# A convolution and two state space layers: half of delta·u·B moved to ScalarE and TensorE, one ring of PSUM work banks, the layer's begin in pieces

## The chip, the cores and the metric

The kernel runs on one NeuronCore of a Trainium2 chip. TensorE (PE) multiplies matrices and transposes 128x128 blocks into PSUM; VectorE (DVE), ScalarE (ACT) and GpSimd (POOL) work on 128 partitions; SyncE (SP) starts DMAs. The metric is the device time of one execution in microseconds (us). All arithmetic is in float32.

## The reference

The input `x` has 4 images of 128 rows, 128 columns and 128 channels. Two residual layers follow one another, each behind a group norm over 32 groups:

```
x = x + L0(gn(x))      # deformable 3x3 sampling, depthwise 3x3, pointwise, 2 channel groups
x = x + L1(gn(x))      # two Mamba blocks over sequences: one image row, 128 positions, 128 channels
```

L0 predicts 18 offsets a position, samples the normed image bilinearly at 9 shifted points, and convolves. A Mamba block with 256 inner channels d and 16 states n computes

```
u, res  = split(h @ in_w);  u = silu(causal_conv4(u) + cb)
dt, B, C = split(u @ xw);   delta = softplus(dt @ dtw + dtb)
s[t,d,n] = exp(delta[t,d] * A[d,n]) * s[t-1,d,n] + delta[t,d]*u[t,d] * B[t,n]
y[t,d]   = sum_n s[t,d,n] * C[t,n] + u[t,d] * D[d]
h        = (y * silu(res)) @ ow
```

The products delta·u·B and the recurrence over t, for 4 x 128 rows, 2 blocks, 256 channels and 16 states, are what the change is about.

## The kernel before

**Layer 0.** `stats_part` reads four rows of x, transposes them and takes their statistics; `norm_part` makes scale and bias; `table_part` writes the normed image to DRAM as a table in which one entry holds the 2x2 neighbourhood of a position (8 writes of 128 KB a part). `prep` computes offsets, weights and indices for 8 rows. Then for each block of 4 rows (32 an image) and each of 9 units, `gather` issues 8 indirect DMAs from GpSimd into two `gt` tiles (`NGT` = 4 buffers), `sample` weights them on DVE (`gw`, line 382), transposes and sums them on PE (`p`) and copies them with ACT (`s`, line 396); for 5 of the 9 units `add_up` (line 415) issues the fused depthwise and pointwise matmuls into `acc`. A float32 matmul appears in the trace as two records, a transpose as one.

**Layer 1.** A job is one block of four image rows (512 positions, `TB`) and one Mamba block: 64 jobs an image, 256 in all. Channels lie on partitions, in two halves c. `pre` computes u, silu(res) (`g`), B and C (stored to DRAM as `bcd`), delta (`de`) and delta·u (`du`); softplus alternates between ACT and DVE (lines 538 to 550). `main` goes through eight steps q of two states n. In a step SP loads B and C of the two states, broadcast to all partitions (`bc`, two times 512 KB); ACT writes exp(delta·A) into one of three `da` tiles (line 580), whose first column of every row is zero so that the recurrence starts anew; DVE multiplies du by B into `hs` (line 586, once a state), runs the recurrence as one scan over 2048 elements (line 592) and multiplies by C (line 596); PE transposes the result into `y` (two PSUM banks), adding all states up (16 transposes a step, helper line 128). After eight steps DVE multiplies by `g` (line 607), PE transposes back and multiplies by `ow`. `pre` of the next job stands ahead of `main` of the present one in the text.

**Order of the work.** Image 0's layer 0 runs alone. After it, layer 0 of image b+1 and layer 1 of image b advance by turns, 288 units against 512 steps, layer 0 a little ahead; layer 1 of image 3 runs alone at the end. Statistics, norm and tables of image b+1 are spread over the units of layer 0 of image b (`todo`). The text of the program gives a priority only: the framework's planner models the engines and issues, on each engine, the earliest instruction in the text among those whose inputs and buffers it takes to be ready. The engines then run their queues in that fixed order. PSUM has eight banks: two for layer 0's work (`ps`), two for `acc` (`psa`), two for layer 1's work (`ps1`), two for `y`.

Of the kernel before, what the change touches and what calls it, by code (L numbers as in the profile page):

```python
# [24 lines left out]
NGT = 4  # L25
# [38 lines left out]
def block_kernel(ctx: ExitStack, tc: tile.TileContext, a: dict, out: bass.AP):  # L64
# [27 lines left out]
    ps = ctx.enter_context(tc.tile_pool(name="l0ps", bufs=2, space=PSUM))  # L92
# [3 lines left out]
    ps1 = ctx.enter_context(tc.tile_pool(name="l1ps", bufs=2, space=PSUM))  # L96
# [39 lines left out]
    dwb = loadw("dwb", [P, NT], pool=p2, tag="ot")  # L136
# [21 lines left out]
    dpar = loadw("dpar", [P, NL, NC], pool=p2, tag="ot")  # L158
# [4 lines left out]
    cvw = loadw("cvw", [P, NL, DCONV, NC * P], pool=p2, tag="hs")  # L163
    for l in range(NL):
        nc.vector.tensor_tensor(
            inc[:, l], cvw[:, l], inw[:, l].unsqueeze(1).to_broadcast([P, DCONV, NC * P]), ALU.mult
        )
# [23 lines left out]
    def norm_part(b):  # L191
# [3 lines left out]
        for nm, v in (("s", scale), ("b", bias)):  # L195
            dg = small.tile([P, P], F32, tag="dg", name=f"dg_{nm}_{b}")
            nc.vector.tensor_scalar(dg, ident, v, None, ALU.mult)
            pr = ps.tile([P, 512], F32, tag="t", name=f"prow_{nm}_{b}")
            nc.tensor.matmul(pr[:, 0:P], ones, dg, start=True, stop=True)
            row = small.tile([P, P], F32, tag=f"row_{nm}", name=f"row_{nm}_{b}")  # L200
            nc.scalar.copy(row, pr[:, 0:P])
            rows.append(row)
# [223 lines left out]
    def layer0(b):  # L426

        todo = []
        if b + 1 < B:
            todo += [lambda j=j: stats_part(b + 1, j) for j in range(NJ)]  # L430
            todo += [lambda: norm_part(b + 1)]
            todo += [lambda j=j: table_part(b + 1, j) for j in range(NJ)]
# [30 lines left out]
    das = [cw.tile([P, NC, NQ, SR, P], F32, name=f"da{i}") for i in range(NDA)]  # L463
# [14 lines left out]
    def load_x1(blk, nm):  # L478
# [3 lines left out]
        return t  # L482

    def pre(st, l):
# [25 lines left out]
        for i in range(SR // 2):  # L510
# [7 lines left out]
            tc.keep_in_program_order(nc.scalar.activation(g[:, 2 * i : 2 * i + 2], px, AF.Silu))  # L518
        pdb = ps1.tile([P, TB], F32, tag="t", name=f"pdb_{nm}")
# [7 lines left out]


        de = p2.tile([P, NC, TB], F32, tag="de", name=f"de_{nm}", bufs=2)
        du = p2.tile([P, NC, TB], F32, tag="du", name=f"du_{nm}", bufs=2)  # L530
        es, pdts = [], []
        for c in range(NC):
# [4 lines left out]
            e = p2.tile([P, TB], F32, tag="e", name=f"e_{nm}_{c}", bufs=2)  # L537
            nc.scalar.activation(e, pdt, AF.Abs)
            nc.scalar.activation(e, e, AF.Exp, scale=-1.0)
            es.append(e)  # L540
            pdts.append(pdt)
        for c in range(NC):
            e = es[c]
            w1 = p2.tile([P, TB], F32, tag="w1", name=f"w1_{nm}_{c}")
            nc.scalar.activation(w1, e, AF.Identity, bias=1.0)
            nc.scalar.activation(du[:, c], w1, AF.Ln)  # L546
            nc.vector.scalar_tensor_tensor(e, w1, 1.0, e, op0=ALU.subtract, op1=ALU.subtract)  # L547
            nc.vector.scalar_tensor_tensor(de[:, c], pdts[c], 0.0, e, op0=ALU.max, op1=ALU.subtract)  # L548
        nc.vector.tensor_tensor(de, de, du, ALU.add)  # L549
        nc.vector.tensor_tensor(du, de, u, ALU.mult)  # L550
        st.update(u=u, g=g, delta=de, du=du, bcd=bcd)

    def main(st, l):
# [5 lines left out]
        for i in range(SR):  # L559
            for c in range(NC):  # L560
# [3 lines left out]
                )  # L564
        for q in range(NS // NQ):
            bc = []
            for w in range(2):
                t = p2.tile([P, NQ, TB], F32, tag=f"bc{w}", name=f"bc{w}_{nm}_{q}", bufs=2)
                n0 = w * NS + q * NQ
                nc.sync.dma_start(t, st["bcd"][n0 : n0 + NQ, :].partition_broadcast(P))  # L570
                bc.append(t)
# [3 lines left out]
            nc.scalar.copy(da.rearrange("p c n s t -> p (c n s) t")[:, :, 0], zero)  # L575
            for c in range(NC):
                dv = st["delta"][:, c].rearrange("p (s t) -> p s t", s=SR)
                for n in range(NQ):
                    s = q * NQ + n
                    nc.scalar.activation(  # L580
                        da[:, c, n, :, 1:], dv[:, :, 1:], AF.Exp, scale=aneg[:, l, c, s : s + 1]
                    )
            hs = p2.tile([P, NC, NQ, TB], F32, tag="hs", name=f"hs_{nm}_{q}")

            for n in range(NQ):
                nc.vector.scalar_tensor_tensor(  # L586
                    hs[:, :, n, :], st["du"], ones[:, 0:1],
                    bc[0][:, n].unsqueeze(1).to_broadcast([P, NC, TB]),
                    op0=ALU.mult, op1=ALU.mult,
                )  # L590
            df = da.rearrange("p c n s t -> p (c n s t)")
            nc.vector.tensor_tensor_scan(  # L592
                df, df, hs.rearrange("p c n t -> p (c n t)"), zero[:, 0:1], ALU.mult, ALU.add
            )
            dc = da.rearrange("p c n s t -> p c (n s t)")
            nc.vector.scalar_tensor_tensor(  # L596
                dc, dc, ones[:, 0:1],
                bc[1].rearrange("p n t -> p (n t)").unsqueeze(1).to_broadcast([P, NC, NQ * TB]),
                op0=ALU.mult, op1=ALU.mult,
            )  # L600
            for c in range(NC):
                for n in range(NQ):
                    for i in range(SR):
                        add_transposed(y[:, i, c], da[:, c, n, i, :], False, q == NS // NQ - 1 and n == NQ - 1)
# [15 lines left out]
        else:  # L620
# [8 lines left out]
            ot = p2.tile([P, SR, P], F32, tag="ot", name=f"ot_{nm}")  # L629
# [11 lines left out]
    def layer1():  # L641
        pre(*jobs[0])
        for i, job in enumerate(jobs):
            if i + 1 < len(jobs):
                pre(*jobs[i + 1])
            yield from main(*job)
# [101 lines left out]
```

## Time and profile before

| | us |
|---|---|
| median of 3 runs | 26,681.26 (26,681.15 to 26,698.94) |
| the profiled execution's own time | 26,698.06 |
| its span | 26,696.0 |
| DVE busy | 23,505.8 (88%) |
| PE busy | 19,620.5 (73%) |
| POOL busy | 16,017.0 (60%) |
| ACT busy | 11,605.1 (43%) |

The first gather starts at 319.7 us, the first scan of layer 1 at 3471.2 us, and the last gather at 21,045.0 us. A group's row gives line, engine, operation, output and inputs with their shapes, the count, then busy us and the mean duration in ns of one, then the idle time of the engine just ahead of such instructions and who ended most of it. A row of a stretch gives, for each engine, its busy us and its number of instructions, then TensorE's granted clock as a share of full speed, the share of time the DMA engines were busy, and GB/s. Time in which an engine waits is not busy, but a GpSimd gather held up while it runs is. Ends of matmuls are modelled, so PE's busy time is somewhat above what its array needs.

### The profile page before, as it was taken

The numbers are of one execution on the slowest core, as the hardware profiler recorded it, in microseconds if no ns is written. First come the engines' busy times: TensorE is split into PE (matmuls) and PEld (weight loads), VectorE is DVE, ScalarE is ACT, GpSimd is POOL, SyncE is SP. The second block draws the span as 40 slices with busy tenths as digits, with TensorE's granted clock in tenths as the row PEclk, the third lists the DMA queues.
The fourth block names the chain that finished last, engine by engine and source line by source line (L and its number), as shares of the span: only waits on it lengthen the run. The fifth ranks groups of instructions, "written<-read, shape, count | busy, mean of one in ns | idle before, by whom it ended". The sixth has DMA issues, their size and how long they took to land. (4 is left out here: it accounts for less than half of the span.)

```text
span 26696.0 us, 294801 instructions
## 1 busy us (share of the span) xinstructions
PE 19620.5 (73%) x112196; PEld 13523.4 (51%) x112196; DVE 23505.8 (88%) x14042; ACT 11605.1 (43%) x18181; POOL 16017.0 (60%) x9222
## 2 busy tenths in 40 slices
PE   4777788878888778887888778888888655555555
PEld 3444455555555555555555555555555443434344
DVE  2232289999999999999999999999999999999999
ACT  0000044444444544444444454444445455555554
POOL 4777777878877767888878667877878400000000
PEclk7888888888999888888998888899998866666666
DMA  5363344456544444455544444444444333333332
GB/s 146 114 172 107 106 147 155 157 170 183 165 153 154 149 144 155 158 173 181 164 154 153 148 143 151 156 150 152 154 154 156 130 107 106 107 106 107 107 106 102
DMA packets 1994602, 3804.53 MB, mean 143 GB/s; under 512 B 771796, under 2 KB 1116116, under 8 KB 1993053
## 3 DMA queue, kind: packets, MB, share of 16 engines
q1 hardware_dynamic: 1550812, 2577.13, 29.9%
q0 software_dynamic: 442368, 1208.55, 14.4%
q8 instruction: 880, 14.42, 0.2%
q14 instruction: 542, 4.43, 0.0%
HBM read 3567.63 MB, written 217.05 MB: 142 GB/s over the span
## 5 line engine op out<-in xcount | busy, mean ns | idle before, releaser
L364 POOL DMA_INDIRECT gt<-table,idx x9216 | 16016.3, 1738 | 5031.5 <-issue 2999.5
L592 DVE TENSOR_TENSOR_SCAN da<-da,zero,hs 128x2048 f32<-128x2048 f32 x2048 | 9176.1, 4481 | 351.7 <-ACT da L580 247.1
L128 PE MATMUL y<-ident,da 128*128 128x128 f32 x32768 | 5252.0, 326 | 3956.1 <-DVE da L596 3955.4
L580 ACT ACTIVATE da<-de,aneg 128x508 f32<-128x508 f32 x8192 | 5550.5, 712 | 5605.2 <-PE y L128 5351.0
L128 PEld LDWEIGHTS y<-ident,da 128*128 128x128 f32 x32768 | 4682.4, 171 | 4953.3 <-DVE da L596 2520.6
L415 PE MATMUL acc<-s,wc 128*64 128x256 f32 (+3 forms) x38400 | 6403.2, 453 | 761.4 <-ACT s L396 760.9
L586 DVE SCALAR_TENSOR_TENSOR hs<-du,ones,bc 128x1024 f32<-128x1024 f32 x4096 | 5093.2, 1277 | 0.0
L415 PEld LDWEIGHTS acc<-s,wc 128*64 128x64 f32 x38400 | 3352.0, 145 | 3083.2 <-issue 1446.2
L596 DVE SCALAR_TENSOR_TENSOR da<-da,ones,bc 128x2048 f32<-128x2048 f32 x2048 | 4807.9, 2348 | 25.9
L382 DVE TENSOR_TENSOR gw<-gt,wt 128x1024 f32<-128x1024 f32 x2304 | 2786.4, 1213 | 2133.3 <-DMA gt<-table,idx 1500.9
L128 PE MATMUL p<-ident,gw 128*128 128x128 f32 x18432 | 2724.3, 299 | 1714.1 <-DVE gw L382 1706.7
L128 PEld LDWEIGHTS p<-ident,gw 128*128 128x128 f32 x18432 | 2292.8, 154 | 2329.3 <-DVE gw L382 1752.7
L396 ACT COPY s<-p 128x512 f32<-128x512 f32 x1152 | 668.6, 581 | 3989.8 <-PE p L128 3982.0
L501 PE MATMUL pu<-hp,inc 128*128 128x512 f32 x4096 | 1808.3, 593 | 0.0
L580 ACT ACT_TABLE_LOAD x1016 | 1303.5, 1283 | 16.8 <-PE y L128 5.7
L501 PEld LDWEIGHTS pu<-hp,inc 128*128 128x128 f32 x4096 | 751.2, 188 | 865.9 <-issue 865.2
L508 ACT ACTIVATE u<-pu,w_cvb 128x512 f32<-128x512 f32 x512 | 324.6, 684 | 1468.9 <-PE y L561 1461.4
L561 PEld LDWEIGHTS y<-ddiag,u 128*128 128x128 f32 x4096 | 579.5, 200 | 192.0 <-issue 192.0
L612 PE MATMUL pyg<-ident,g 128*128 128x128 f32 x2048 | 353.9, 328 | 425.7 <-DVE g L607 424.8
L546 ACT ACT_TABLE_LOAD x500 | 641.5, 1283 | 8.9
L561 PE MATMUL y<-ddiag,u 128*128 128x128 f32 x4096 | 612.1, 284 | 0.0
L263 PE MATMUL pof<-xn,w_offw 128*64 128x512 f32 x2304 | 585.0, 613 | 20.0 <-ACT xn L257 12.0
(118 smaller groups left out, 11036.3 us busy)
## 6 DMA issues: line engine op xcount, KB each, us to landing
bc<-bcd SPq DMA_DIRECT2D x4096, 512.0 KB
gt<-table,idx POOLq DMA_INDIRECT x9216
table<-xt SPq DMA_DIRECT2D x984, 128.0 KB
xt<-in_x SPq DMA_DIRECT2D x124, 320.0 KB
xr<-in_x SPq DMA_DIRECT2D x128, 256.0 KB
x<-xo SPq DMA_DIRECT2D x128, 256.0 KB
x1t<-x SPq DMA_DIRECT2D x128, 256.0 KB
x1t_o<-x SPq DMA_DIRECT2D x128, 256.0 KB
```

The lines of the kernel that those rows point to most:

```text
L128: nc.tensor.matmul(o, v, ident, is_transpose=True, start=start, stop=stop, skip_group_check=True)
L364: nc.gpsimd.indirect_dma_start(out=gt[:, v, r], out_offset=None, in_=flat, in_offset=bass.IndirectOffsetOnAxis(ap=idx[:, ri, o : o + 1], a ...
L382: nc.vector.tensor_tensor(gw.rearrange("p r s v c -> p (r s) v c"), gts[h].rearrange("p v r (s c) -> p (r s) v c", c=CG), wv.unsqueeze(3). ...
L396: nc.scalar.copy(st[:, :, 1 : W + 1], p4)
L415: nc.tensor.matmul(accs[b, j + i0][CG * g : CG * g + CG, q : q + rb - ra, :], wc[sl, v, e, :], st[p + 4 * g if p < 4 else 8][sl, ra:rb, kx ...
L501: nc.tensor.matmul(px.rearrange("p (s t) -> p s t", s=SR), inc[:, l, j, c * P : (c + 1) * P], h[:, :, j : j + P], start=(j == 0), stop=(j ...
L546: nc.scalar.activation(du[:, c], w1, AF.Ln)
L561: nc.tensor.matmul(y[:, i, c], st["u"][:, c, i * P : (i + 1) * P], ddiag[:, l, c, :], start=(i % 2 == 0 and c == 0), stop=False, skip_grou ...
L580: nc.scalar.activation(da[:, c, n, :, 1:], dv[:, :, 1:], AF.Exp, scale=aneg[:, l, c, s : s + 1])
L586: nc.vector.scalar_tensor_tensor(hs[:, :, n, :], st["du"], ones[:, 0:1], bc[0][:, n].unsqueeze(1).to_broadcast([P, NC, TB]), op0=ALU.mult, ...
L592: nc.vector.tensor_tensor_scan(df, df, hs.rearrange("p c n t -> p (c n t)"), zero[:, 0:1], ALU.mult, ALU.add)
L596: nc.vector.scalar_tensor_tensor(dc, dc, ones[:, 0:1], bc[1].rearrange("p n t -> p (n t)").unsqueeze(1).to_broadcast([P, NC, NQ * TB]), op ...
```

## The change

- In every step the product delta·u·B of the second state is no longer made by DVE. `pre` transposes `du` once a job (`dut`: positions on partitions) and B likewise (`bt`); in the transposed form B is one number a partition, so ACT multiplies 128x256 pieces by it (`xs`, four a state), and PE transposes them back into one PSUM bank (`psx`), from where the scan reads them, once for each half c.
- The scan of a step is split: the first state from `hs` as before (1024 elements), the second in two scans of 512 from PSUM. B is loaded for the first state only (`bs`), C for both (`cs`).
- For image 3 (`in_last`), whose layer 1 runs alone, GpSimd makes `xs` of the first state as well, `hs` and `bs` are gone, all four scans read PSUM, and two of them use the two `acc` banks, which are free then.
- The multiply by C is a `tensor_tensor` in place of a `scalar_tensor_tensor` with a factor of one.
- `pre` becomes a generator of pieces, run after the steps of the previous job. Softplus is done by ACT on both halves together, max(x,0) by a Relu; DVE's part (four instructions on 1024 elements) comes two steps later.
- One ring of three PSUM banks serves both layers' work in place of two and two; `NGT` is 3 in place of 4.
- Statistics, norms and tables of images 1, 2 and 3 are all spread over layer 0 of image 0.
- Some tiles change the tag under which they share memory; one weight load (`cvw`) comes in two halves.

```diff
-NGT = 4
+NGT = 3
...
-    ps = ctx.enter_context(tc.tile_pool(name="l0ps", bufs=2, space=PSUM))
+    ps = ctx.enter_context(tc.tile_pool(name="ps", bufs=3, space=PSUM))
...
-    ps1 = ctx.enter_context(tc.tile_pool(name="l1ps", bufs=2, space=PSUM))
+    ps1 = ps
+    psx = ctx.enter_context(tc.tile_pool(name="l1psx", bufs=1, space=PSUM))
...
     for l in range(NL):
+        cvw = p2.tile([P, DCONV, NC * P], F32, tag="hs", name=f"w_cvw_{l}")
+        nc.sync.dma_start(cvw, a["cvw"][:, l])
...
-        if b + 1 < B:
-            todo += [lambda j=j: stats_part(b + 1, j) for j in range(NJ)]
-            todo += [lambda: norm_part(b + 1)]
-            todo += [lambda j=j: table_part(b + 1, j) for j in range(NJ)]
+        for i in range(1, B) if b == 0 else ():
+            todo += [lambda i=i, j=j: stats_part(i, j) for j in range(NJ)]
+            todo += [lambda i=i: norm_part(i)]
+            todo += [lambda i=i, j=j: table_part(i, j) for j in range(NJ)]
...
+    def in_last(blk):
+
+        return blk * SR // H == B - 1
...
             tc.keep_in_program_order(nc.scalar.activation(g[:, 2 * i : 2 * i + 2], px, AF.Silu))
+        yield
...
+        pbt = ps1.tile([P, SR, XP], F32, tag="t", name=f"pbt_{nm}")
+        for i in range(SR):
+            nc.tensor.transpose(pbt[:, i, :], dbl[:, i * P : (i + 1) * P], ident[0:XP, 0:XP])
+        st["bt"] = p2.tile([P, SR, NS], F32, tag="bt", name=f"bt_{nm}", bufs=2)
+        nc.scalar.copy(st["bt"], pbt[:, :, DTR + 1 : DTR + 1 + NS])
+        yield
...
-            e = p2.tile([P, TB], F32, tag="e", name=f"e_{nm}_{c}", bufs=2)
-            nc.scalar.activation(e, pdt, AF.Abs)
-            nc.scalar.activation(e, e, AF.Exp, scale=-1.0)
-            es.append(e)
-            pdts.append(pdt)
-        for c in range(NC):
-            e = es[c]
-            w1 = p2.tile([P, TB], F32, tag="w1", name=f"w1_{nm}_{c}")
-            nc.scalar.activation(w1, e, AF.Identity, bias=1.0)
-            nc.scalar.activation(du[:, c], w1, AF.Ln)
-            nc.vector.scalar_tensor_tensor(e, w1, 1.0, e, op0=ALU.subtract, op1=ALU.subtract)
-            nc.vector.scalar_tensor_tensor(de[:, c], pdts[c], 0.0, e, op0=ALU.max, op1=ALU.subtract)
+            nc.scalar.activation(e[:, c], pdt, AF.Abs)
+            nc.scalar.activation(de[:, c], pdt, AF.Relu)
+        nc.scalar.activation(e, e, AF.Exp, scale=-1.0)
+        nc.scalar.activation(w1, e, AF.Identity, bias=1.0)
+        nc.scalar.activation(du, w1, AF.Ln)
+        nc.scalar.activation(w1, w1, AF.Identity, bias=-1.0)
+        yield
+        yield
+        nc.vector.tensor_tensor(e, w1, e, ALU.subtract)
+        nc.vector.tensor_tensor(de, de, e, ALU.subtract)
         nc.vector.tensor_tensor(de, de, du, ALU.add)
         nc.vector.tensor_tensor(du, de, u, ALU.mult)
+        dut = p2.tile([P, SR, NC * P], F32, tag="dut", name=f"dut_{nm}", bufs=2)
+        for k in range(SR // 2):
+            pt = ps1.tile([P, 2, NC, P], F32, tag="t", name=f"pdu_{nm}_{k}")
+            for i in range(2):
+                for c in range(NC):
+                    o = (2 * k + i) * P
+                    nc.tensor.transpose(pt[:, i, c, :], du[:, c, o : o + P], ident)
+            nc.scalar.copy(dut[:, 2 * k : 2 * k + 2], pt.rearrange("p s c d -> p s (c d)"))
...
+            turned = {}
+            for n in range(0 if last else 1, NQ):
+                s = q * NQ + n
+                for i in range(SR):
+                    if i % 2 == 0:
+                        xs = p2.tile([P, 2, NC * P], F32, tag="xs", name=f"xs_{nm}_{s}_{i}", bufs=3)
+                        turned[n, i] = xs
+                    bv = st["bt"][:, i, s : s + 1]
+                    if n:
+                        nc.scalar.activation(xs[:, i % 2], st["dut"][:, i], AF.Copy, scale=bv)
+                    else:
+                        nc.gpsimd.tensor_scalar(xs[:, i % 2], st["dut"][:, i], bv, None, ALU.mult)
+
+            def scan_turned(n, c):
+                pool, tag = (psa, "acc") if last and (n + c) % 2 else (psx, "x")
+                px = pool.tile([P, SR, P], F32, tag=tag, name=f"px_{nm}_{q}_{n}_{c}")
+                for i in range(SR):
+                    nc.tensor.transpose(px[:, i, :], turned[n, i - i % 2][:, i % 2, c * P : (c + 1) * P], ident)
+                dn = da[:, n, c].rearrange("p s t -> p (s t)")
+                nc.vector.tensor_tensor_scan(dn, dn, px.rearrange("p s t -> p (s t)"), 0.0, ALU.mult, ALU.add)
+
+            if last:
+                for n in range(NQ):
+                    for c in range(NC):
+                        scan_turned(n, c)
+            else:
+
+                hs = p2.tile([P, NC, TB], F32, tag="hs", name=f"hs_{nm}_{q}")
                 nc.vector.scalar_tensor_tensor(
-                    hs[:, :, n, :], st["du"], ones[:, 0:1],
-                    bc[0][:, n].unsqueeze(1).to_broadcast([P, NC, TB]),
+                    hs, st["du"], ones[:, 0:1], bs.unsqueeze(1).to_broadcast([P, NC, TB]),
                     op0=ALU.mult, op1=ALU.mult,
                 )
...
+                scan_turned(1, 0)
+                d0 = da[:, 0].rearrange("p c s t -> p (c s t)")
+                nc.vector.tensor_tensor_scan(
+                    d0, d0, hs.rearrange("p c t -> p (c t)"), 0.0, ALU.mult, ALU.add
+                )
+                scan_turned(1, 1)
+            dc = da.rearrange("p n c s t -> p n c (s t)")
+            nc.vector.tensor_tensor(dc, dc, cs.unsqueeze(2).to_broadcast([P, NQ, NC, TB]), ALU.mult)
...
     def layer1():
-        pre(*jobs[0])
+        for _ in pre(*jobs[0]):
+            pass
         for i, job in enumerate(jobs):
-            if i + 1 < len(jobs):
-                pre(*jobs[i + 1])
-            yield from main(*job)
+
+            nxt = pre(*jobs[i + 1]) if i + 1 < len(jobs) else iter(())
+            for _ in main(*job):
+                next(nxt, None)
+                yield
+            for _ in nxt:
+                pass
```

## The prediction

> **What bounds the kernel now.** I read the 40 slices first, for stages, then one table of busy times by stage, then the costliest groups, the waits, and the order of time where a wait needed its cause.
>
> ```profile
> DVE  2232289999999999999999999999999999999999
> POOL 4777777878877767888878667877878400000000
> PEclk7888888888999888888998888899998866666666
> ```
>
> Three stages show. In A (0 to 3430 us) image 0's layer 0 runs alone, with GpSimd (POOL) the busiest of the vector engines and VectorE (DVE) at 2 tenths. In B (to 21,050 us, the last gather) layer 1 of images 0 to 2 runs beside layer 0 of images 1 to 3. In C layer 1 of image 3 runs alone, and TensorE's granted clock drops.
>
> ```profile
> core 0: us, PE busy (x) PEld busy (x) DVE busy (x) ACT busy (x) POOL busy (x), PEclk, DMA share, GB/s
> 400.00:2400.00 2000.00, 1590.65 (x9911) 970.70 (x9912) 582.10 (x674) 151.50 (x268) 1548.25 (x1484) 0.88 0.47 132
> 5400.00:21000.00 15600.00, 12500.77 (x73564) 8599.82 (x73563) 15247.58 (x9079) 7541.39 (x11893) 12047.88 (x6101) 0.89 0.49 157
> 22000.00:26000.00 4000.00, 2097.48 (x9502) 1603.67 (x9500) 3798.31 (x1871) 2038.60 (x3096) 0.00 (x0) 0.70 0.31 107
> ```
>
> DVE is busy 97.7% of B and 95% of C: it is the bound of both. TensorE (PE) is at 80% in B, ScalarE (ACT) at 48% in B and 51% in C. Stage A is paced by POOL: 1484 gathers in 2000 us, 1.35 us each. The scan counts by stage give the number of state steps (two of the 16 states each):
>
> ```profile
> 3430.00:21050.00 17620.00, 6755.10 (x1508) 0.89 0.49 157
> 21050.00:26696.00 5646.00, 2421.01 (x540) 0.70 0.31 106
> ```
>
> So a step costs 17,620 / 1508 = 11.68 us in B and 10.46 in C. What DVE spends it on:
>
> ```profile
> L592 DVE TENSOR_TENSOR_SCAN da<-da,zero,hs 128x2048 f32<-128x2048 f32 x2048 | 9176.1, 4481 | 351.7 <-ACT da L580 247.1
> L586 DVE SCALAR_TENSOR_TENSOR hs<-du,ones,bc 128x1024 f32<-128x1024 f32 x4096 | 5093.2, 1277 | 0.0
> L596 DVE SCALAR_TENSOR_TENSOR da<-da,ones,bc 128x2048 f32<-128x2048 f32 x2048 | 4807.9, 2348 | 25.9
> L382 DVE TENSOR_TENSOR gw<-gt,wt 128x1024 f32<-128x1024 f32 x2304 | 2786.4, 1213 | 2133.3 <-DMA gt<-table,idx 1500.9
> ```
>
> The idle columns say that DVE hardly waits for anyone once layer 1 runs; the longest wait of C is for ScalarE's exponentials where layers meet (table of waits of C):
>
> ```profile
> DVE da L592 <- ACT da L580: 151.3, 48, 5.6
> ```
>
> That cover is what the change spends: PE and ACT now enter DVE's own chain, so their queues matter. The order of time shows PE's queue in B:
>
> ```profile
> 8061.95 4.48 DVE L592 TENSOR_TENSOR_SCAN da<-da,zero,hs 128x2048 f32<-128x2048 f32 x1
> 8062.57 7.97 PE L415 MATMUL acc<-s,wc 128*64 128x256 f32 x56
> 8063.16 4.03 POOL L364 DMA_INDIRECT gt<-table,idx  x1 [0.30 <-issue]
> 8070.47 1.96 PE L128 MATMUL y<-ident,da 128*128 128x128 f32 x16
> 8071.21 1.94 ACT L580 ACTIVATE da<-de,aneg 128x508 f32<-128x508 f32 x3 [8.97 <-PE y L128]
> ```
>
> Layer 0's add_up goes through PE in one piece of 8 us; the transposes of y stand behind it, and ACT waits 9 us for them. DVE does not feel it, as three da buffers lie between.
>
> **The change, part by part.**
>
> *DVE work of a step in B.* One of two hs multiplies goes: two in a row take 2.47 us, one 1.28, so -1.19. The multiply by C becomes a plain tensor_tensor; at 1024 elements that form has 1.214 us against 1.277, so -0.07. One scan of 2048 (4.48) becomes one of 1024 and two of 512 that read PSUM, which the trace lacks. L586 and L596 give a DVE instruction a fixed part of about 0.21 us; with that the scan costs 2.09 ns per element, so 2.34 + 2 x 1.27 = 4.89; neighbours overlap by 0.08 us (2 x 1.277 against 2.47). I take +0.25, between +0.2 and +0.45 (no overlap where the scan waits for PE). Reading PSUM is nearly free by a row: 682 ns at L548 (input in PSUM) against 678 at L547. Softplus: four instructions of 0.68 become two of about 1.21, -0.3 a layer, -0.04 a step. Statistics and tables of images 2 and 3 leave B: 64 x (0.69 + 0.82 + 0.81) = 148 us, -0.10 a step. Sum -1.15; times 1508, **-1,735 us**.
>
> *Waits it adds in B.* The scans of the second state use one PSUM bank: four transposes, scan, four transposes, scan. Ahead of the first lie the C multiply and hs (3.5 us) as cover, ahead of the second only the scan of 1024 (2.3 us). Four transposes need about 0.7 us, so PE is in time unless it is inside an add_up. Each add_up has 30 matmuls (60 records); there are 5 a row block, 160 an image, 480 in B. If an 8 us piece starts just before the second four, DVE waits 8 + 0.7 - 2.3 = 6.4 us; if it starts just after them, the scan of 1024, scan, multiply and next hs (7 us) hide all but 1.7. DVE can also fill in gw (2.4 us a unit). I take 2 us each, bounds 0 and 6.4: **+960** (0 to 3,070). PE itself has room: y's 16 transposes take 1.96 us, so 8 more are 1 us a step, and the turned du and B add 0.15; busy 9.4 of 11.7 becomes 10.5 of about 11.2, so little slack remains. ACT gains four multiplies of 256 elements a step; nearest row is the 128x260 copy, 0.405 us, so 0.4 to 0.5 each, plus some 3 us a layer (two Relus, two copies of the turned du, less work on joined tiles) and minus two table loads of 1.283: 5.6 us a step becomes about 7.3, hidden.
>
> *GpSimd and DMA in B.* A gather beside a scan waits for its end, above; beside DVE work that reads PSUM it does not:
>
> ```profile
> 4221.39 1.21 DVE L607 TENSOR_TENSOR g<-y,g 128x1024 f32<-128x1024 f32 x1
> 4221.45 0.95 POOL L364 DMA_INDIRECT gt<-table,idx  x1 [0.30 <-issue]
> ```
>
> So the short scans should free POOL, which now needs 1.97 + 0.3 us a gather, 15,700 of 17,620. With three gather buffers in place of four this hides at nothing; if POOL is not freed, it fills 93% of the shorter stage and gw comes late, up to +300. B is broadcast for one state, not two: 256 of 1024 KB a step go, from a queue that was not awaited. Three work banks for both layers instead of two and two: some 2.3 tiles a step with 3 to 4 us each are one bank in use on average; hidden, up to +200 if not.
>
> *Stage C.* Both hs go (-2.47), four scans of 512 in place of 4.48 (+0.45), the multiply -0.07: -2.09 a step, -16.7 a layer, with softplus -17. A layer of C takes 4000 / 48 = 83.3 us, 79.1 of it DVE; DVE falls to 62. ACT, 42.5 a layer, gains 32 x 0.4 to 0.5 and the 3 us, less 2.6: 55.5 to 58, over 90% of that. The other half is turned by GpSimd: four multiplies of 256 elements a step; the nearest POOL row is a select of 128 elements, 0.29 us, so 0.4 to 0.6 each, far under a step. DVE's idle time of 4.2 us a layer I raise to 7, because ACT works in blocks and xs has three buffers: 69 us, -14.3; times 64, **-915**, and -30 for the 28 steps that still have image 2's form.
>
> [...] The rows: 16 transposes take 1.96 us in B, but in C
>
> ```profile
> 24000.36 3.37 PE L128 MATMUL y<-ident,da 128*128 128x128 f32 x16 [5.75 <-DVE da L596]
> ```
>
> behind 5.75 us of idleness. They do run at full rate in B; whether a stage that is mostly transposes raises its own clock is not shown. [...]
>
> *Stage A* takes the 64 parts of images 2 and 3. With table traffic (1400 to 1800 us) 291 gathers started in 400 us, otherwise 300: 3% over some 450 us an image, +28. DMA share was 0.77 there, so packing three images' tables in stays under one. With three buffers a gather waits for the gw two tiles (10 us) back, which is done. The split weight load adds some 10. **+40**, up to +300.
>
> Sum: -1,735 + 960 - 945 + 40 = -1,680, from the profiled 26,698 to 25,018; the median run is 17 below it: **25,000 us**, own range 24,400 to 25,700.
>
> **Rivals.**
> 1. *No new waits*: the scheduler places transposes well. B -1,735, C -17 x 64 = -1,090: 23,860. For it: PE has 20% free. Against: the 8 us piece ahead of y.
> 2. *PE eats stage B's gain*, waits of 3.6 us an add_up, or C runs at the cold clock: 25,700 to 26,500, centre 26,000.
> 3. *Slower*: DVE waits at the single bank. Place: second four transposes behind add_up; price 6.4 us x 480 = 3,070, and C gains 600 only as ACT or PE binds: 26,681 + 1,335 - 600 + 40 = 27,450. It decides from (1,735 + 945 - 40) / 480 = 5.5 us an add_up. For it: ACT's 9 us above. Against: gw work fills, and nearly every piece must fall badly.
> 4. *It does not do what it says* for time: gains and waits cancel within 0.2% (53 us, about what a measurement can tell), 26,680.
>
> **How the numbers follow.** Chances: forecast 0.48, no waits 0.12, B eaten 0.20, slower 0.17, cancel 0.03. So faster 0.80, same 0.03, slower 0.17. The range 23,900 to 26,900 leaves out half of rival 1 and most of rival 3.
>
> **What would show it.** Right: scans of 512 at 1.2 to 1.35 us; DVE waiting for transposes some 1,000 us in B, mostly behind L415's successor; ACT above 85% busy in C; gathers' mean below 1.7 us; stage A ending near 3,470; granted clock of C near 0.8. Wrong: DVE's wait for transposes above 2,600 us, gw waiting for gathers by hundreds, C's clock at 0.7 with PE the last to end, or a scan from PSUM well above 1.4 us.

## The result, and the profile after

The changed kernel takes **28,220.88 us** (median of 4 runs, 28,203.61 to 28,242.33) where the kernel before takes 26,685.15 (4 runs beside them): a ratio of **1.0575, 95% interval 1.0557 to 1.0593**. It is slower by 5.8%. The forecast was 25,000, its range ended at 26,900; both missed, and in sign.

The profiled execution took 28,215.46 us, its span is 28,213.7. First the slices of the page of the changed kernel, each about 705 us long:

```profile
PE   5778788888888788888888788888888777777777
DVE  2333388888888888888888888888888866666666
POOL 4777765655555365655555365655555344444444
PEclk7889899999999899999999899999999888888888
```

The row of DVE had nines from slice 7 to the end, and now has eights in B (layer 1 beside layer 0) and sixes in C (layer 1 of image 3 alone). DVE has less to do and the kernel takes longer, so DVE stands idle more than before. The same three stretches as before the change (the third lies later because stage C begins later):

```profile
core 0: us, PE busy (x) PEld busy (x) DVE busy (x) ACT busy (x) POOL busy (x), PEclk, DMA share, GB/s
400.00:2400.00 2000.00, 1601.97 (x10153) 983.31 (x10149) 665.63 (x796) 152.61 (x273) 1546.73 (x1484) 0.89 0.59 160
5400.00:21000.00 15600.00, 13018.78 (x80708) 9278.54 (x80707) 12804.31 (x9304) 8874.47 (x16101) 8856.96 (x5704) 0.92 0.39 121
24000.00:28000.00 4000.00, 2951.97 (x15210) 2275.76 (x15210) 2747.16 (x2029) 2429.17 (x4302) 1822.10 (x1444) 0.82 0.16 53
```

In B DVE went from 15,248 to 12,804 us busy in 15,600, and no other engine is full: PE has 83%. In C nobody is above 74%. Where no engine is busy all the time, what sets the pace must be looked for in the waits between engines.

Cut at the first scan and the last gather, the spans are these (a step is two states of one layer job; "busy" and "idle" are DVE's time in a step):

| stage | before, us | after, us | forecast of the difference | difference | before: step, busy, idle | after: step, busy, idle |
|---|---|---|---|---|---|---|
| A | 3,471 | 3,485 | +40 | +14 | | |
| B (1,507 steps) | 17,578 | 18,728 | -775 | +1,150 | 11.66, 11.39, 0.27 | 12.43, 10.21, 2.22 |
| C (541 steps) | 5,647 | 6,001 | -945 | +354 | 10.44, 9.89, 0.55 | 11.09, 7.67, 3.42 |

The groups that are new or altered, from the changed kernel's page (busy us and mean ns of one, then the idle time just ahead and who ended most of it):

```profile
L627 DVE TENSOR_TENSOR_SCAN da<-da,px 128x512 f32<-128x512 f32 x5120 | 6150.2, 1211 | 3116.7 <-PE px L625 3104.5
L617 ACT ACTIVATE xs<-dut,bt 128x256 f32<-128x256 f32 x8192 | 3671.4, 498 | 2270.8 <-PE px L625 2261.0
L647 DVE TENSOR_TENSOR da<-da,cs 128x2048 f32<-128x2048 f32 x2048 | 4675.1, 2283 | 28.7
L619 POOL TENSOR_SCALAR xs<-dut,bt 128x256 f32<-128x256 f32 x2048 | 2587.4, 1275 | 3386.4 <-PE px L625 2780.3
L642 DVE TENSOR_TENSOR_SCAN da<-da,hs 128x1024 f32<-128x1024 f32 x1536 | 3497.2, 2277 | 797.4 <-ACT da L598 451.0
```

Every duration on DVE is near what the forecast had for it. The idle column is not: 3,104 us of DVE's time go by ahead of the scans from PSUM, until TensorE's transposes (L625) have written the bank. DVE's waits in 5,400 to 21,000 us and then in 24,000 to 28,000 us (us in total, times, longest):

```profile
DVE da L627 <- PE px L625: 1193.7, 590, 8.9
DVE gw L384 <- PE p L129: 459.9, 175, 5.1
DVE da L642 <- ACT da L598: 376.7, 190, 3.9
DVE da L642 <- ACT da L603: 260.3, 102, 7.1
DVE gw L384 <- DMA gt<-table,idx: 171.1, 62, 4.9
```

```profile
DVE da L627 <- PE px L625: 1148.6, 566, 14.0
DVE g L654 <- PE y L129: 98.6, 45, 2.2
```

In C the wait for the turned states is nearly the whole idle time (1,149 of 1,253 us). In B it is 1,194 of 2,796 us: the waits for what ScalarE writes into `da` (the zero columns of L598 and the exponentials of L603, 377 and 260 us; both are called exponentials below) and for the transposes of the samples (460) grew as well. Before the change these were, in the same 15,600 us:

```profile
DVE da L592 <- ACT da L580: 34.5, 18, 5.0
DVE gw L382 <- PE p L128: 21.3, 33, 1.0
```

What a long wait looks like is seen when one engine at a time is read in order of time. DVE, then TensorE, in the same 16 us of stage B:

```profile
12535.48 1.21 DVE L627 TENSOR_TENSOR_SCAN da<-da,px 128x512 f32<-128x512 f32 x1
12544.62 1.22 DVE L627 TENSOR_TENSOR_SCAN da<-da,px 128x512 f32<-128x512 f32 x1 [7.94 <-PE px L625]
```

```profile
12534.74 0.60 PE L625 MATMUL px<-ident,xs 128*128 128x128 f32 x4
12535.39 8.61 PE L265 MATMUL pof<-xn,w_offw 128*64 128x512 f32 x36
12543.93 0.66 PE L625 MATMUL px<-ident,xs 128*128 128x128 f32 x4
```

The second four transposes write the bank that the first scan still reads until 12,536.7. In TensorE's fixed queue an 8.6 us piece of layer 0 (the offset convolution) stands between the two fours, and DVE waits 7.94 us. The scan of 1024, which stands between these two scans in the text of the kernel, is not between them here. The second four start as the 36 records of the offset convolution end: at 12,543.93, where those run to 12,544.00.

### The profile page after: what moved, and what is told of

The parts are those of the page before. It is cut to its first block, busy times and chain, and to the rows that moved or that the text cites. A ratio compares the mean times of both kernels' runs of the same rounds, so it can differ in the third digit from the quotient of the medians.

```text
span 28213.7 us, 356586 instructions
## 1 busy us (share of the span) xinstructions
PE 22604.8 (80%) x135748; PEld 16114.0 (57%) x135748; DVE 20651.1 (73%) x15578; ACT 14555.3 (52%) x26241; POOL 15735.4 (56%) x11270
## 4 chain that ended last, share of the span: by engine, by line
PE 30%; DVE 22%; issue 20%; POOL 20%; ACT 4%; DMA 3%; SPq 1%; DVEq 0%; POOLq 0%; ACTq 0%
POOL gt L366 16%; PE y L129 9%; DVE da L627 7%; DVE da L647 5%; PE acc L417 4%; POOL xs L619 4%; PE pu L507 4%; PE px L625 4%; DVE da L642 3%; DMA gt<-table,idx 2%; DVE hs L636 2%; DVE gw L384 2%; PE p L129 2%; PE pof L265 1%; ACT da L603 1%
## 5 line engine op out<-in xcount | busy, mean ns | idle before, releaser
L366 POOL DMA_INDIRECT gt<-table,idx x9216 | 13147.3, 1427 | 9064.6 <-DVE gw L384 6081.4
L627 DVE TENSOR_TENSOR_SCAN da<-da,px 128x512 f32<-128x512 f32 x5120 | 6150.2, 1211 | 3116.7 <-PE px L625 3104.5
L603 ACT ACTIVATE da<-de,aneg 128x508 f32<-128x508 f32 x8192 | 5524.2, 712 | 4627.1 <-PE y L129 4429.5
L417 PE MATMUL acc<-s,wc 128*64 128x256 f32 (+3 forms) x38400 | 6086.3, 435 | 188.4 <-ACT s L398 183.0
L625 PE MATMUL px<-ident,xs 128*128 128x128 f32 x20480 | 3745.4, 307 | 2810.4 <-DVE da L627 1509.3
L625 PEld LDWEIGHTS px<-ident,xs 128*128 128x128 f32 x20480 | 2577.6, 155 | 4353.3 <-DVE da L627 1601.3
L617 ACT ACTIVATE xs<-dut,bt 128x256 f32<-128x256 f32 x8192 | 3671.4, 498 | 2270.8 <-PE px L625 2261.0
L647 DVE TENSOR_TENSOR da<-da,cs 128x2048 f32<-128x2048 f32 x2048 | 4675.1, 2283 | 28.7
L619 POOL TENSOR_SCALAR xs<-dut,bt 128x256 f32<-128x256 f32 x2048 | 2587.4, 1275 | 3386.4 <-PE px L625 2780.3
L642 DVE TENSOR_TENSOR_SCAN da<-da,hs 128x1024 f32<-128x1024 f32 x1536 | 3497.2, 2277 | 797.4 <-ACT da L598 451.0
L636 DVE SCALAR_TENSOR_TENSOR hs<-du,ones,bs 128x1024 f32<-128x1024 f32 x1536 | 1963.7, 1278 | 20.2
```

The costliest lines, as they stand in the source:

```text
L366: nc.gpsimd.indirect_dma_start(out=gt[:, v, r], out_offset=None, in_=flat, in_offset=bass.IndirectOffsetOnAxis(ap=idx[:, ri, o : o + 1], a ...
L417: nc.tensor.matmul(accs[b, j + i0][CG * g : CG * g + CG, q : q + rb - ra, :], wc[sl, v, e, :], st[p + 4 * g if p < 4 else 8][sl, ra:rb, kx ...
L603: nc.scalar.activation(da[:, n, c, :, 1:], dv[:, :, 1:], AF.Exp, scale=aneg[:, l, c, s : s + 1])
L617: nc.scalar.activation(xs[:, i % 2], st["dut"][:, i], AF.Copy, scale=bv)
L619: nc.gpsimd.tensor_scalar(xs[:, i % 2], st["dut"][:, i], bv, None, ALU.mult)
L625: nc.tensor.transpose(px[:, i, :], turned[n, i - i % 2][:, i % 2, c * P : (c + 1) * P], ident)
```

## The experiments

Letters in the quoted expectations: Q is the wait for the turned states at TensorE's queue and bank, G the multiplies of GpSimd, R the rest of the change, N the gather buffers; others are explained where they stand. The first three kernels ran on a chip on which the kernel before took 27,370.34 us, and all three show a stage A of about 4,180 us in place of 3,485. So of these three the ratio and the stages B and C are used, not the total. On the chips of the other nine it took 26,694 to 26,705 us.

**1. No wait for the turned states.** The scan of a turned state takes its data from SBUF (`du` without the factor B), so DVE waits for no transpose and no transpose waits for a scan; all multiplies and transposes still run. Left out: the factor B of these states.

```diff
-    nc.vector.tensor_tensor_scan(dn, dn, px.rearrange("p s t -> p (s t)"), 0.0, ALU.mult, ALU.add)
+    nc.vector.tensor_tensor_scan(dn, dn, st["du"][:, c], 0.0, ALU.mult, ALU.add)
```

> The changed kernel, but the scans of the turned states read du in SBUF in place of the PSUM bank (so those states lack the factor B); every transpose, every multiply on ScalarE and GpSimd and the bank itself stay. Theory Q (VectorE waits because the transposes into the one bank stand behind other work in TensorE's fixed queue): without that wait VectorE goes at its own pace, 10.2 us of work a step and under 0.6 us idle, so stage B takes 16,000 to 16,500 us (18,731 in the changed kernel), stage C 4,300 to 5,200 (6,003), and the whole 24,000 to 25,200. Theory R (the rest of the change costs the time: ring of three banks, three gather buffers, pieces): VectorE still idles 2 us a step in B and the whole stays above 27,500. Theory L (TensorE is simply full): the whole stays above 27,000 with TensorE above 88% busy.

Measured: ratio 0.9776 (0.9747 to 0.9804); B 17,045 us, C 5,497. Waiting on the round trip through PSUM is what turns the gain into a loss, but not all that was missed: B stays above theory Q's 16,000 to 16,500, with DVE still waiting, in 5,400 to 21,000 us:

```profile
DVE gw L384 <- DMA gt<-table,idx: 478.0, 169, 5.8
DVE da L627 <- ACT da L603: 460.3, 142, 13.5
```

and C stays above 4,300 to 5,200. There DVE waits for ScalarE, which waits for TensorE to release `xs` tiles, while TensorE waits for GpSimd (988 us of 4,000 between 22,500 and 26,500). The edit has a side effect: with data from SBUF the mean gather of B takes 1.87 us in place of 1.56, so part of the wait for gathers may be its own.

**2. Image 3 as the others**: GpSimd makes nothing, DVE makes the first state's `hs` again.

```diff
     def in_last(blk):
-        return blk * SR // H == B - 1
+        return False
```

> The changed kernel, but image 3 is done as the other images are: the first state of a step by VectorE out of SBUF, no multiply on GpSimd, one bank, not three. Theory G (in stage C the multiplies on GpSimd, 0.92 us alone and up to 4 us beside VectorE's multiply, hold up the ring of three xs tiles): C falls from 11.08 us a step to 9 to 9.7, so the whole loses 700 to 1,050 us, to 27,150 to 27,500. Theory Q alone (TensorE's queue sets C too): VectorE's work rises by 0.4 us a step and only one bank is left, so C stays at 10.8 to 11.5 and the whole at 28,000 to 28,450. Stage B stays at 18,700 +- 150 in both.

Measured: ratio 1.0475 (1.0445 to 1.0506); C 5,563 us, 10.3 us a step, with DVE busy 8.68 of it. Handing GpSimd's half back to DVE gives DVE 1 us a step more to do and makes C 438 us shorter than in the changed kernel. It lies between the two expectations, so GpSimd is part of C's loss and not shown to be all. B, which this edit does not touch, is 18,937 us here against 18,728, outside the 150 allowed for it; stage times from this chip can be off by some 200 us.

**3. All but the turned path.** `hs` of both states by DVE and one scan of 2048, as before; the pieces of `pre`, softplus, tables, the ring of three banks, three gather buffers and the plain multiply by C stay.

```diff
-            turned = {}
...
-            def scan_turned(n, c):
...
+            for n in range(NQ):
+                nc.vector.scalar_tensor_tensor(hs[:, n], st["du"], ones[:, 0:1], ...)
+            nc.vector.tensor_tensor_scan(d0, d0, hs.rearrange("p n c t -> p (n c t)"), ...)
```

> The changed kernel without its first part: both states are multiplied by B on VectorE into hs and scanned at once over 2048 elements, with B loaded for both states, as before; no turned du, no turned B, no fourth bank. All else of the change stays: ring of three banks for both layers, three gather buffers, layer begun in pieces, softplus on joined halves, tensor_tensor for the multiply by C, statistics and tables in stage A. Theories Q and G: the loss goes, and the small savings of VectorE stay: B 11.45 to 11.6 us a step, C 10.2 to 10.4, stage A 3,480: 26,250 to 26,550, 0.5 to 1.6% under the kernel before. Theory R (the rest costs the time): over 27,300.

Measured: ratio 1.0113 (1.0083 to 1.0142), where a gain of 0.5 to 1.6% was expected. C is better than before (5,371 against 5,647), B is worse (18,149 against 17,578, on the other chip), and DVE waits 809 us, 326 times, for gathers in 5,400 to 21,000 us, where the kernel before waited 98 us. So something in the rest costs as well.

**4 and 5. Three gather buffers alone, and the rest with four.** The kernel before with `NGT` at 3 (the diff), and the kernel of experiment 3 with `NGT` at 4.

```diff
-NGT = 4
+NGT = 3
```

> The kernel before with three gather buffers in place of four, nothing else. If three are enough, as the prediction took it: stage B stays at 11.6 to 11.75 us a step and the ratio to the kernel before at 1.000 +- 0.004. If the gathers are pressed (theory N: a gather must wait for gw two tiles back while VectorE's scans hold it up): VectorE waits for gathers 500 us or more in B, as in the run without the turned path, B 12.0 to 12.2 us a step, ratio 1.015 to 1.03.

> The run without the turned path (all else of the change), with four gather buffers again. Theory N: VectorE's wait for gathers in B falls from 800 us to under 150, B from 12.04 to 11.4 to 11.6 us a step, C stays at 9.95: ratio 0.970 to 0.990. If the wait came from the ring of three banks or from the order of the pieces, B stays above 11.9 and the ratio above 1.005.

Measured: the kernel before with three buffers has a ratio of **1.0198** (1.0168 to 1.0228), 27,230.81 us; its stage B is 527 us longer and the other stages move by 13 us at most. The rest of the change with four has **0.9895** (0.9866 to 0.9924), 26,422.38 us. DVE's wait for gathers in 5,400 to 21,000 us, before, then with three:

```profile
DVE gw L382 <- DMA gt<-table,idx: 98.1, 43, 4.2
```

```profile
DVE gw L382 <- DMA gt<-table,idx: 545.7, 236, 4.0
```

Both kernels agree: about 2% for one buffer (1.0113 against 0.9895 is 2.2%, the two on different chips). Experiment 5 still waits 345 us for gathers where under 150 was expected, and its B of 11.64 us a step is just above theory N's. The reordered `pre` with ScalarE's softplus and the plain multiply by C seem worth something by themselves: in experiment 5 C is 265 us shorter, of which only 0.11 us a step (60 us) is less DVE work; the rest is DVE's idle time, 0.55 us a step before and 0.16 now.

**6. The transposes first.** In TensorE's order the transposes into `px` stand 400 instructions further ahead than their place in the text.

```diff
-                for i in range(SR):
+                with tc.high_priority(400):
+                  for i in range(SR):
                     nc.tensor.transpose(px[:, i, :], ...)
```

> The changed kernel with the transposes into the bank moved ahead by 400 instructions in the planner's priority, so that they go before add_up and y where both are ready; nothing else. Theory Q: the planner puts them ahead, VectorE's wait for px in B falls from 1,190 us to under 700 in the same stretch and B from 12.43 to 11.7 to 12.2 us a step. If TensorE's whole load is the limit (theory L), other waits take its place and B stays at 12.3 to 12.6.

Measured: ratio 1.0279 (1.025 to 1.0309); B 18,204 us, 524 less. DVE's wait for `px` in 5,400 to 21,000 us falls from 1,194 to 90 us, but its wait for exponentials rises from 637 to 1,337, and TensorE now stands at the head of its own queue (its longest group of waits in the same stretch, the changed kernel, then this one, whose lines count one higher):

```profile
PE px L625 <- DVE da L627: 1164.2, 910, 6.6
```

```profile
PE px L626 <- DVE da L628: 1934.2, 1904, 5.5
```

Put first, the second four wait for the bank, and all the work of TensorE behind them waits too. So most of the wait was moved, and less than half of B's loss came back (524 of 1,150 us).

**7. No multiplies.** `px` is transposed straight from the turned `du`; ScalarE and GpSimd multiply nothing. Left out: the factor B of the turned states.

```diff
-            for n in range(0 if last else 1, NQ):
+            for n in ():
...
-    nc.tensor.transpose(px[:, i, :], turned[n, i - i % 2][:, i % 2, c * P : (c + 1) * P], ident)
+    nc.tensor.transpose(px[:, i, :], st["dut"][:, i, c * P : (c + 1) * P], ident)
```

> The changed kernel with the transposes into the bank reading the turned du itself: no multiplies by B on ScalarE and GpSimd and no xs tiles (the turned states lack the factor B); transposes, bank, scans as in the change. Theory Q: B stays at 12.0 to 12.4 us a step, since TensorE's queue and the bank are as before. Theory G: C, freed of GpSimd and of the ring of three xs tiles, falls from 11.09 to 8 to 9 us a step. If ScalarE's load were what holds B, B falls below 11.5.

Measured: ratio 1.0324 (1.0294 to 1.0354). B stays at 18,761 us (33 more than in the changed kernel) and C falls to 5,317 (684 less). This parts the two stages: ScalarE's multiplies cost B nothing, and with the multiplies and their tiles gone C is 330 us shorter than before the change. But theory G expected 8 to 9 us a step in C, and it is 9.8: the multiplies are not all that holds C.

**8. Four work banks** in place of three, on top of experiment 5.

```diff
-    ps = ctx.enter_context(tc.tile_pool(name="ps", bufs=3, space=PSUM))
+    ps = ctx.enter_context(tc.tile_pool(name="ps", bufs=4, space=PSUM))
-    psx = ctx.enter_context(tc.tile_pool(name="l1psx", bufs=1, space=PSUM))
```

> As e5 (all of the change but the turned path, four gather buffers), with four work banks of PSUM in the common ring in place of three; the bank of the turned states isn't there. Theory H (as predicted, a ring of three is hidden): within 0.3% of e5, 26,340 to 26,500 us, ratio 0.987 to 0.993. Theory K (three banks hold PE up): stage B falls by a further 100 to 300 us, 26,100 to 26,330 us, ratio 0.978 to 0.986, and DVE's waits for gathers (345 us in e5) fall with it.

Measured: 26,408.31 us, ratio 0.9894 (0.9877 to 0.991): no difference from experiment 5. Three banks are as good as four in this kernel, which has no turned path.

**9. No multiply by GpSimd**: in image 3 ScalarE makes `xs` of both states.

```diff
-                    if n:
+                    if True:
                         nc.scalar.activation(xs[:, i % 2], st["dut"][:, i], AF.Copy, scale=bv)
```

> The changed kernel, but in image 3 ScalarE multiplies both states by B and GpSimd none. Theory P (GpSimd's multiplies and the three tiles behind them set stage C): C falls from 6,001 to 5,350 to 5,650 us, ratio to the kernel before 1.032 to 1.045, stage B as it was (18,600 to 18,850). Rival T (ScalarE has no room for 4 x 0.5 us more a step, 6.7 of 11.1 us now and 8.7 then): ScalarE over 90% busy in C, C 5,800 to 6,200, ratio 1.050 to 1.065.

Measured: ratio 1.0264 (1.0243 to 1.0284). B is 18,727 us, as it was; C falls from 6,001 to **5,166** us, further than theory P expected. Four multiplies more a step fit into ScalarE (83% busy in C). The stretch of 23,000 to 27,000 us:

```profile
23000.00:27000.00 4000.00, 2994.78 (x17787) 2229.25 (x17786) 3162.49 (x2374) 3400.85 (x6716) 0.00 (x0) 0.92 0.19 62
```

What slowed GpSimd there is seen in the changed kernel's order of time; GpSimd, then DVE:

```profile
25508.36 1.82 POOL L619 TENSOR_SCALAR xs<-dut,bt 128x256 f32<-128x256 f32 x2 [3.20 <-PE px L625]
25511.28 3.58 POOL L619 TENSOR_SCALAR xs<-dut,bt 128x256 f32<-128x256 f32 x2 [1.10 <-PE px L625]
```

```profile
25511.81 2.27 DVE L647 TENSOR_TENSOR da<-da,cs 128x2048 f32<-128x2048 f32 x1
```

Two multiplies take 1.82 us beside scans from PSUM and 3.58 where DVE multiplies two tiles of SBUF; the median is 922 ns, the longest single one 4,068.

**10. Two banks for the turned states**, and two work banks in place of three.

```diff
-    ps = ctx.enter_context(tc.tile_pool(name="ps", bufs=3, space=PSUM))
+    ps = ctx.enter_context(tc.tile_pool(name="ps", bufs=2, space=PSUM))
-    psx = ctx.enter_context(tc.tile_pool(name="l1psx", bufs=1, space=PSUM))
+    psx = ctx.enter_context(tc.tile_pool(name="l1psx", bufs=2, space=PSUM))
```

> The changed kernel with two PSUM banks for the turned states and two work banks in place of one and three. Theory S (the single bank makes DVE wait: the second four transposes can't start before the first scan has read): DVE's waits for px in 5,400 to 21,000 us fall from 1,194 to under 400 us, B from 18,728 to 17,600 to 18,000, ratio 1.015 to 1.035. Theory O (the order of PE's queue makes it wait: the four stand behind other matmuls whatever bank they write): px waits stay over 900 us, B within 200 us of 18,728, ratio 1.050 to 1.065; the lost work bank can add up to 300 us.

Measured: **26,791.57 us, ratio 1.0034** (1.0019 to 1.005), 1,430 us less than the changed kernel and somewhat beyond theory S's 1.015 to 1.035. B falls to 17,586 us, C to 5,721. DVE's waits in 5,400 to 21,000 us:

```profile
DVE da L642 <- ACT da L598: 566.5, 110, 9.0
DVE da L642 <- ACT da L603: 419.9, 139, 7.4
DVE gw L384 <- PE p L129: 394.2, 162, 5.4
DVE da L627 <- PE px L625: 214.1, 90, 6.4
```

The wait for the turned states falls from 1,194 to 214 us, while the waits for exponentials grow from 637 to 986. One bank more, taken from the common ring, gives back 1,142 us of stage B, whatever the smaller ring may cost included. Counted in the traces, in stage B up to 21,000 us, TensorE's two fours of a step follow one another with nothing between in 1,285 of 1,502 steps, in the changed kernel in 75 of 1,409. With a second bank the planner mostly leaves them together.

**11. Two banks and first in order**: experiments 6 and 10 together.

> As e6 (transposes of the turned states placed ahead in TensorE's order) with two PSUM banks for them and two work banks. Order and bank together: theory S says that in e6 TensorE stood 1,934 us at the head of its queue waiting for DVE to free the bank, and that ends: B falls from 18,204 to 17,200 to 17,700, total 26,600 to 27,000, ratio 0.996 to 1.012. Theory O: order was all, B stays 18,000 to 18,400, ratio 1.022 to 1.035.

Measured: ratio 1.0272 (1.0251 to 1.0293), B 18,316 us. That is within theory O's numbers, but O itself (order is all) fell with experiment 10, and S, which took the priority to help, fell here: against experiment 10 it costs 730 us of B. TensorE again stands waiting for DVE ahead of `px`, 1,838 us in 5,400 to 21,000. With the bank doubled, the planner's own order is better than this one.

**12. Two banks and no multiply by GpSimd**: experiments 9 and 10 together.

> e9 and e10 together: two PSUM banks for the turned states, two work banks, and in image 3 ScalarE multiplies both states by B. If the two causes are separate (one bank in B and partly C, GpSimd in C), the gains add: stage B as in e10 (17,586), C about 5,721 - 835 = 4,890 (at most 5,166, e9's), total 25,970 to 26,250 us, ratio 0.973 to 0.983, which would be the fastest of all. Rival: in C ScalarE (83% busy in e9) or TensorE is the next bound and little adds: C 5,150 to 5,300, total 26,250 to 26,400, ratio 0.983 to 0.989. What three gather buffers cost stays in either.

Measured: **26,230.62 us** (4 runs, 26,213.03 to 26,249.71), **ratio 0.9826** (0.981 to 0.9843): the fastest of the kernels that do all the work, 475 us (1.7%) under the 26,705.46 of the kernel before in the runs beside it. B is 17,543 us as in experiment 10, C 5,174 as in experiment 9. So the two edits act in separate stages: the bank in B, GpSimd in C. In C the gains do not add: 4,890 us was expected, and 5,174 is what the rival named. What binds C next, ScalarE, TensorE or the order, is not shown. Three rows of its slices, of which the last seven lie wholly in C:

```profile
PE   4777788888888888888888888888888877778777
DVE  2333368888888898888888898888888887777777
ACT  0000045665655665665665665665665678888888
```

## Why the prediction was wrong

**The work was counted rightly.** DVE's busy time a step in B fell by 1.18 us (1.15 forecast), a layer of C to 61.4 us (62), the scan of 512 from PSUM takes 1.211 us (1.27 taken, 1.2 to 1.35 named), stage A ended at 3,485 (near 3,470), the gathers' mean in B fell to 1.56 us (below 1.7). All the sums of removed and added DVE instructions hold. What failed is time in which DVE does nothing: 1.95 us a step or +2,940 us in B against +960, and 27.4 us a layer in C against 7.

**The step that failed first: "Waits it adds in B", 2 us for each of 480 add_ups, +960 us in all.** It counted one wait, at the single bank, and put the others at nothing. The one that it counted was about a third larger than taken. In the whole of B:

```profile
DVE da L627 <- PE px L625: 1430.3, 708, 8.9
```

That is 3.0 us an add_up; experiment 10 shows what the single bank costs B, 1,142 us. Two assumptions made this term too small. Any long piece of TensorE's queue can fall between the two fours, not add_up alone: the offset convolution above does. And the cover ahead of the second four, "only the scan of 1024 (2.3 us)", is mostly not there: the planner put that scan elsewhere in 1,123 of the 1,507 steps of B, and 968 of the 1,430 us are waited in these steps, ahead of the second scan. And `gw` fills a gap only where DVE's fixed order has it: in the lines above the scan is DVE's next instruction, whatever else could run.

The larger failure is what was put at nothing. With two banks, B takes 17,586 us, where the forecast's saving of work without any wait would give 17,578 - 1,735 = 15,843. DVE is then idle for 1.53 us a step, against 0.27 before the change: 1,900 us more in B. The waits that grew are those for ScalarE's exponentials (986 us in 15,600, against 35 before) and for the samples' transposes (394, against 21). The forecast had seen ScalarE wait 9 us behind the transposes of `y` and took three `da` tiles to cover it; in the changed kernel they do not.

Rival 3 had the sign and the place (the second four at the single bank), and its +1,335 us for B is near the +1,150 measured. In part that is luck: it came to its number by 3,070 us of waits at the bank, and 1,430 were there; the rest of the 2,940 came from waits that it did not name. The sign named for it, waits for the transposes above 2,600 us, shows in the page (3,104), but 1,674 of these lie in C. Its 27,450 was still 771 us short, since it let C gain 600 where C lost 354.

**The step that failed second: GpSimd's multiplies, "0.4 to 0.6 each, far under a step".** They measure 1.275 us in the mean, 0.92 in the median. The row they were taken from, a select of 128 elements, was no near row. Four of them, 5.1 us a step, are still under a step of 11.1; what was missed besides the size is that the scans stand behind them. A pair that takes 1.82 us beside scans from PSUM takes 3.58 beside the multiply by C (experiment 9). In the changed kernel's whole trace 1,362 multiplies run beside no multiply by C and take 0.92 us in the median, 1.965 at most; the 686 beside one take 1.735, 4.068 at most. The forecast had GpSimd held up by DVE in gathers only (4.03 us beside a scan). The lateness went on to TensorE, which waits 799 us for GpSimd in 4,000 us of C, and to DVE. Experiment 9 shows its size: 835 of the 1,299 us by which C missed its forecast.

**The step that failed third: three gather buffers, where it says "this hides at nothing".** The argument looked at the one gather that waits for the `gw` two tiles back, and not at what four buffers had absorbed. Experiment 4 measures 535 us on the kernel before, above the stated bound of 300. A likely reason, not tested apart, is that a gather took 4.03 us beside a long scan and 0.95 beside DVE work that reads PSUM, and that a stock of gathered tiles bridges this. On the changed kernel four buffers were not tried. There DVE waits only 171 us for gathers in 15,600, so what the missing buffer costs it stays open.

**Stage C** was to be near 69 us a layer with ScalarE above 85% busy. Without GpSimd and with two banks it is 9.56 us a step or 76.5 a layer, ScalarE at 82%, DVE at 79%: even then the round trip is not hidden (DVE idles 16 us a layer, 7 were forecast), and its waits come seldom and long, in 22,000 to 26,000 us:

```profile
DVE da L627 <- PE px L625: 768.9, 87, 14.9
```

What sets them was not taken apart.

**The clock of C.** The forecast named a granted clock near 0.8 there, and that was right: it was 0.70 before the change and 0.82 after it, with 2,952 us of TensorE's work in 4,000 in place of 2,097. What the change adds to TensorE is transposes alone, 16 a step and some in `pre`; in experiment 9, with the same transposes in less time, the clock was 0.92. What raises it is not shown. In the trace before the change the 16 transposes of `y` take 1.965 us in the median where the granted clock is 1.0 throughout (753 groups in B) and 3.65 where it is 0.5 (171 in 22,000 to 26,000 us). Rival 2 let C run at a "cold clock", which can be read as the 0.70 from before; no run shows the price it put on that, and the changed kernel shows 0.82.

**What held:** the ring of three banks costs nothing that shows (experiment 8, without the turned path); ScalarE's multiplies, 498 ns each, are hidden in B (experiment 7). The forecast priced no gain of idle time for the rest of the change: with four gather buffers and no turned path, it gains 1.05% in all.

**What stays open in B.** With two banks DVE has 1.25 us a step less to do than before, and B is as long as before. TensorE is busy for 87% of it, and one gather buffer is missing, at a cost not measured there. Whether these stand behind the added waits, or the order of the queues does, was not told apart.

## What to carry to other kernels

Where a change moves work from an engine that is full into a loop over other engines, count the buffers on the way first: a producer and a consumer that share one buffer must take turns, and here each turn could cost a long piece of other work that the planner had put between (8.61 us in the lines of stage B above). Take the cover of a wait from the order in which the instructions are issued, not from the text of the program. A wait at one place is not the whole price: ask what else stands behind the waiting engines, because waits that were covered before may be felt afterwards. Take the duration of an operation only from a row of the same operation at that size, and see what runs beside it.

## What was not expected of the hardware

- A scan of 512 elements takes 1.211 us with its data in PSUM and 1.240 with them in SBUF (experiment 1): reading PSUM costs a scan no time that shows.
- GpSimd's multiply of 128x256 elements by a column takes 0.92 us in the median and up to 4.07; ScalarE does the same in 0.498.
- TensorE's granted clock in C was 0.70 before, 0.82 after, 0.89 in experiment 7 and 0.92 in experiment 9, although TensorE is busy for 74 to 76% of the time in the last three. Busy share alone doesn't give the clock; what does is not shown here.
- Less work was not less time: C is 5,317 us without any multiply (experiment 7) and 5,166 with all of them on ScalarE (experiment 9). Whether the order that the planner gave each of them is the reason stays open.
